# Shorter warm-up products, key weights split by head pair, ScalarE in the centring of Wq, and a later row gather in a gated cross-attention block

## The chip, the cores and the metric

The kernel runs on one core of a Trainium2 chip. The metric is the device time of one execution in microseconds (us); the median of three runs of the kernel before is 1246.3 us (1245.36 to 1249.04). Engines are named as in the profile: PE is TensorE (PEld its weight loads), DVE is VectorE, ACT is ScalarE, POOL is GpSimd, SP issues most of the DMAs.

## The reference

`x` has 4 batches of 2048 tokens of 512 features, all in float32. The context has 77 keys of 384 features for each batch, and there are 16 heads of 64.

```
q = split_heads(layernorm(x) @ Wq);  k, v = split_heads(ctx @ Wk), split_heads(ctx @ Wv)
attn = softmax(q k^T / 8)                      # over 77 keys
x = x + tanh(g_xattn) * ((attn @ v) @ Wo + bo)
idx = argmax(log_softmax(logits) - log(-log(u)))      # one of 8 matrices, chosen from data
x = x + tanh(g_ffn) * (layernorm(x) @ W[idx] + b[idx])
```

## The kernel before

The 8192 tokens are cut into 16 groups of 512. Attention is rearranged so that nothing of width 1024 is made for each token: for each batch a matrix `m` (Wq of a head times the keys of that head) gives the scores straight from the 512 features, and a matrix `vo` (the values of a head times Wo) gives the output straight from the softmax weights. Every large product of a group (`ps_s` scores, `ps_a` attention output, `ps_f` the feed-forward) is done with seven block products in place of eight (class `Seven`, its matmuls are line 466); POOL forms the sums and differences of blocks that this needs (`weight_sum` line 123 for the weights, `Columns.sum` line 437 for the tokens).

Ahead of the 16 groups stands a setup stage, and all of the change lies in it. The order of every engine's queue is written out by hand, in program order; PSUM is a ring of seven banks (`bank`), so that a product can start only when the bank used seven allocations earlier has been copied out. The setup runs on PE in this order:

- three products of a zeroed tile with itself (`ps_w`, line 167), which need no input;
- the keys, `project_k`: for each of 8 head pairs three matmuls over 384 features and 308 columns (4 batches of 77 keys), `ps_kv`, line 270; ACT copies each result out (line 275). Beside it `centre_wq` takes the mean of each row of Wq away: DVE sums a row (line 287), scales the sum (288) and writes half of the centred matrix (295), POOL writes the other half (293). The first half (`wqp[0]`) is used by the next step, the second half 20 us later;
- `build_m(0)`: 32 matmuls (`ps_m`, line 300), each with two copies out (lines 306 and 307), half of the heads by ACT and half by DVE;
- the values, `project_v` (`ps_kv` again): 24 matmuls of 320 columns, because the keys were first copied into a tile `cT` padded with zeros to 80 keys a batch; one copy out each (line 280), by ACT and DVE in turn. Between them stand the small steps that choose the feed-forward matrix: `gates0`, `gates1` and `gates2`, the last of them 12 small DVE instructions (lines 229 to 241) that end in the row numbers `rows_u`;
- `build_m(2)` like the first, then `build_vo` for head pairs 0 to 2 (`ps_vo`, line 336, copied out by ACT and DVE, lines 339 and 341) and the stores of `m` and `vo` to DRAM through SP;
- the score products of group 0. In between stands `mean_wf` (line 659), one product that needs the sum of the four chosen row blocks of W.

These row blocks come by `gather` (lines 246 to 251): five indirect DMAs that POOL issues once `rows_u` is there, behind the three block sums of `m` (line 123). `sum_wf` (lines 623 to 625) adds them up on POOL, behind the scaling of `bf_r` (line 251), which waits for the last of the five.

Weights of keys are loaded in four DMAs of 256 columns each, alternately from ACT's and SP's queue; SP then loads Wq in eight DMAs, Wv in four, and x. There are eight completion semaphores for these DMAs, used in turn, so that the ninth DMA is issued only when the first has landed.

Of the kernel before, what the change touches and what calls it, by code (L numbers as in the profile page):

```python
# [8 lines left out]
F32 = mybir.dt.float32  # L9
U32 = mybir.dt.uint32  # L10
AF = mybir.ActivationFunctionType
ALU = mybir.AluOpType
AX = mybir.AxisListType

P = 128
# [4 lines left out]
def flamingo_block_kernel(  # L20
# [33 lines left out]
    nc = tc.nc  # L54
    NT, D = x.shape
    CD, BJ = ctxT.shape
    ID = WqT.shape[0]
    OPS = b.shape[0]
    B = 4
    J = BJ // B  # L60
    H = 16
    DH = ID // H
    NP = H // 2
    NA = 4
    HA = H // NA
    R = 32 // HA
    NK = 2 * ((J + 2 * R - 1) // (2 * R))
    KH = NK // 2
    JP = NK * R
    BP = B * JP  # L70
    NDC = D // P
    NCC = CD // P
    T = 512
    T2 = T // 2
# [6 lines left out]
    wp = ctx.enter_context(tc.tile_pool(name="work", bufs=1))  # L81
# [6 lines left out]
    def bank(name):  # L88
        return pm.tile([P, 512], F32, tag="mm", name=name)
# [10 lines left out]
    tq = cp.tile([P, 4, NDC // 2, T2], F32, tag="tq")  # L100
# [13 lines left out]
    def flat(t):  # L114
        n = len(t.shape) - 1
        names = " ".join("abcdef"[:n])
        return t.rearrange(f"p {names} -> p ({names})")
# [14 lines left out]
    def row_tile(name):  # L132
        return wp.tile([P, NG, P], F32, tag="row", name=name, bufs=3)
# [1 line left out]
    def column_tile(name):  # L135
        return wp.tile([P, NDC, T], F32, tag="xc", name=name, bufs=3)

    cT = wp.tile([P, NCC, B, JP], F32, tag="row", name="cT", bufs=3)
    s_f = flat(wp.tile([P, HA, NG, JP], F32, tag="s", name="m_st"))
    cR = s_f[:, : NCC * BJ].rearrange("p (c b j) -> p c b j", c=NCC, b=B)  # L140
    wv = snap.rearrange("p (c f) -> p c f", c=NCC)
    wk = m_f[:, 4 * 2 * KH * P :][:, : NCC * ID].rearrange("p (c f) -> p c f", c=NCC)
    t = wp.tile([P, NK * T + KH * T2], F32, tag="pT", name="wq")
# [8 lines left out]
    def load(i):  # L152
        xg[i] = row_tile("xg")
        for a in range(NA):
            nc.sync.dma_start(out=xg[i][ts(a, 32)], in_=rows_of(x, i)[:, :, ts(a, P)])

    def load_ctx(c, queue):
        queue.dma_start(out=cR[:, c].rearrange("p b j -> p (b j)"), in_=ctxT[ts(c, P), :])

    def load_w(t, w, h, queue):  # L160
        queue.dma_start(out=t[:, :, ts(h, ID // 4)], in_=w[:, ts(h, ID // 4)].rearrange("(c p) f -> p c f", p=P))

    nc.vector.memset(tq[:, 0], 0.0)
    idle = tq[:, 0].rearrange("p n t -> p (n t)")
    for _ in range(3):
        ps = bank("ps_w")
        nc.tensor.matmul(ps, idle[:, :P], idle, start=True, stop=True)  # L167
    load_ctx(0, nc.sync)
    load_ctx(2, nc.scalar)
    load_ctx(1, nc.sync)  # L170
    load_w(wk, Wk, 0, nc.scalar)
    load_w(wk, Wk, 1, nc.sync)
    load_w(wk, Wk, 2, nc.scalar)
    load_w(wk, Wk, 3, nc.sync)
    nc.gpsimd.memset(cT[:, :, :, J:], 0.0)
    for c in range(NCC):
        nc.vector.tensor_copy(cT[:, c, :, :J], cR[:, c])
    for p in range(NP):
        nc.sync.dma_start(out=wq[:, p, :], in_=WqT[ts(p, P), :])
    for h in range(4):  # L180
        load_w(wv, Wv, h, nc.sync)
    load(0)
    load(1)

# [43 lines left out]
    def gates2():  # L228
        nc.vector.tensor_scalar(z, z, st[:, 2:3], None, ALU.subtract)
        nc.vector.tensor_tensor(z, z, l2, ALU.subtract)  # L230
        nc.vector.tensor_reduce(st[:, 3:4], z, AX.X, ALU.max)

        nc.vector.tensor_scalar(ez, z, st[:, 3:4], None, ALU.is_equal)
        nc.vector.tensor_tensor(ez, ez, rev, ALU.mult)
        nc.vector.tensor_reduce(st[:, 4:5], ez, AX.X, ALU.max)
        nc.vector.tensor_scalar(st[:, 5:6], st[:, 4:5], -1.0, float(OPS), ALU.mult, ALU.add)
        nc.vector.tensor_scalar(st[:, 6:7], st[:, 5:6], float(D), None, ALU.mult)
        nc.vector.tensor_scalar(st[:, 7:8], st[:, 5:6], float(NA), None, ALU.mult)
        nc.vector.tensor_scalar(rows[:, :NDC], rows[:, :NDC], st[:, 6:7], None, ALU.add)
        nc.vector.tensor_scalar(rows[:, NDC:], rows[:, NDC:], st[:, 7:8], None, ALU.add)  # L240
        nc.vector.tensor_copy(rows_u, rows)
    def gather():
        t = row_tile("wfr").rearrange("p g j -> p (g j)").rearrange("p (c d) -> p c d", c=NDC)
        for c in range(NDC):
            at = bass.IndirectOffsetOnAxis(ap=rows_u[:, c : c + 1], axis=0)
            nc.gpsimd.indirect_dma_start(out=t[:, c, :], out_offset=None, in_=W, in_offset=at)
        at = bass.IndirectOffsetOnAxis(ap=rows_u[:, NDC:], axis=0)
        nc.gpsimd.indirect_dma_start(out=bf_r, out_offset=None,
                                     in_=b.rearrange("o (a j) -> (o a) j", j=P), in_offset=at)
        nc.gpsimd.tensor_scalar(bo_c, bo_c, tgx, None, ALU.mult)  # L250
        nc.gpsimd.tensor_scalar(bf_r, bf_r, tgf, None, ALU.mult)
        return t
# [6 lines left out]
    vT = [v_cols(p, 0, BP).rearrange("p (r b k) -> p r b k", b=B, r=R) for p in range(NP)]  # L259
# [3 lines left out]
    kT_f = kT.rearrange("p n b k r -> p n b (k r)")  # L263
    nc.gpsimd.memset(kT_f[:, :, :, J:], 0.0)

    def project(w, p, keys):
        n = keys.shape[2] * keys.shape[3]
        ps = bank("ps_kv")
        for c in range(NCC):
            nc.tensor.matmul(ps[:, :n], w[:, c, ts(p, P)], keys[:, c].rearrange("p b j -> p (b j)"),  # L270
                             start=(c == 0), stop=(c == NCC - 1))
        return ps[:, :n]

    def project_k(p):
        nc.scalar.copy(kT_f[:, p, :, :J], project(wk, p, cR).rearrange("p (b j) -> p b j", b=B))

    def project_v(p):
        d = vT[p].rearrange("p r b k -> p b k r")
        copy = nc.vector.tensor_copy if p % 2 else nc.scalar.copy
        copy(d, project(wv, p, cT).rearrange("p (b k r) -> p b k r", b=B, r=R))  # L280


    wqp = [wp.tile([P, 2, NP, P], F32, tag="xc", name="wqp", bufs=3) for _ in range(2)]
    wqm = cp.tile([P, NP], F32, tag="wqm")

    def centre_wq(p):
        nc.vector.tensor_reduce(wqm[:, p : p + 1], wq[:, p, :], AX.X, ALU.add)
        nc.vector.tensor_scalar(wqm[:, p : p + 1], wqm[:, p : p + 1], -1.0 / D, None, ALU.mult)
        for h in range(2):
            src = by_chunk(wq[:, p, :])[:, ts(h, 2)]  # L290
            dst = wqp[h][:, :, p, :].rearrange("p q (a e) -> p q a e", a=NA)
            if h:
                nc.gpsimd.tensor_scalar(dst, src, wqm[:, p : p + 1], None, ALU.add)
            else:
                nc.vector.tensor_scalar(dst, src, wqm[:, p : p + 1], None, ALU.add)

    def m_head(q, h, stage):
        p, r = h // 2, ts(h % 2, DH)
# [28 lines left out]
    def build_vo(p, engines):  # L327
        n = 0
        for c in range(3):
            r = min(P, BP - c * P)  # L330
            for hh in range(2):
                stg = stage_of(2 * p + hh)
                hr = ts(hh, DH)
                ps = bank("ps_vo")

                nc.tensor.matmul(ps, v_cols(p, c * P, P)[hr], wo[hr, p, :], start=True, stop=True)  # L336
                src, dst = by_chunk(ps[:r, :]), chunked(stg[:r, c, :])
                if engines[n % len(engines)] == "D":
                    nc.vector.tensor_scalar(dst, src, tgx[:r], None, ALU.mult)
                else:  # L340
                    nc.scalar.activation(dst, src, AF.Copy, scale=tgx[:r])
                n += 1
        for hh in range(2):
            d, stg = vo_d[2 * p + hh], stage_of(2 * p + hh)
            nc.sync.dma_start(out=d[0 : 2 * P].rearrange("(c r) e -> r c e", r=P), in_=stg[:, 0:2])
            nc.sync.dma_start(out=d[2 * P :], in_=stg[: BP - 2 * P, 2])
# [257 lines left out]
              (m_f[:, 4 * 2 * KH * P :], vo_f, vo_f[:, NP * D :], s_f)]  # L604
    wo = wq_f.rearrange("p (n e) -> p n e", n=NP)
    norms[0] = Norms(0)
    for p in range(NP):
        project_k(p)
        centre_wq(p)
    nc.gpsimd.dma_start(out=gg[:, 0:1], in_=g_xattn.partition_broadcast(P))  # L610
    nc.gpsimd.dma_start(out=gg[:, 1:2], in_=g_ffn.partition_broadcast(P))
    nc.gpsimd.dma_start(out=lg, in_=logits.partition_broadcast(P))
# [17 lines left out]
    for p in range(NP):  # L630
        project_v(p)
        if p == 0:
            x_columns(0)
            for t in ("T1", "T2", "T3", "T4"):
                xc[0].sum(t)
            weight_sum(m, 0)
        if p == 2:
            gates0()
        if p == 3:
            gates1()  # L640
        if p == 4:
            norms[0].stats(xg[0], 0, 0, NG)
        if p == 6:
            gates2()
    build_m(2, stages[2:])
    store_m(2, stages[2])
    for n in range(1, 4):
        weight_sum(m, n)
    wfr = gather()
    build_vo(0, "AD")  # L650
    store_m(3, stages[3])
    for p in range(1, 3):
        build_vo(p, "AD")

    wf_mean = wf_f[:, ds(5 * D, D)]

# [30 lines left out]
    n = norms[0]  # L687
# [114 lines left out]
    for i in range(1, NGRP):  # L802
        j, f, nx = i - 1, i - 2, i + 1
        n = norms[i]
# [128 lines left out]
        for s in range(6):  # L933
# [16 lines left out]
            if 2 <= s:  # L950
                k = (0, 2, 3, 5, 6)
# [5 lines left out]
    j, f = NGRP - 1, NGRP - 2  # L957
    n = norms[NGRP] = Norms(NGRP)
# [76 lines left out]
    for s in range(6):  # L1035
# [23 lines left out]
        if s == 5:  # L1059
            f_rows(j, ff, 0, 0)  # L1060
            t = by_feature(ts_[j], 0, 0)
# [50 lines left out]
```

## Time and profile before

| | |
|---|---|
| runs of before | 1245.36, 1246.3, 1249.04 us |
| the profiled execution's own time | 1246.03 us |
| its span, first to last instruction | 1244.2 us |
| PE busy | 1234.0 us, 99% of the span |
| setup up to the first score product | 57.8 us |
| HBM traffic | 64 GB/s over the span; 284 GB/s in the first 36 us |

The profile is that of one execution. In a timeline row the first number is the start in us from the beginning of the span, the second the time that the merged instructions took together; the bracket at the end names the idle time before them and what ended it. In the chain of work the pieces follow one another without a gap: that is the path that sets the end. Each float32 matmul of the program appears as two records on PE.

### The profile page before, as it was taken

The page shows a single profiled execution, that of the slowest core. Times are in us where ns is not written, and L with a number is a line of the kernel's source. Part 1 is how long each engine was busy: PE and PEld are TensorE (multiplying, and loading weights), DVE is VectorE, ACT ScalarE, POOL GpSimd, SP SyncE. Part 2 cuts the span into 40 slices and gives each one's busy share as a digit, 9 for nine tenths or more (in the row PEclk, how much of TensorE's full clock was granted, in tenths as well). Part 3 has the DMA queues.
Part 4 walks back from the last instruction along what each step waited for, and adds up shares of the span by engine and source line. Part 5 has one row for each costly group of instructions (what it writes and reads, how often), then busy time and mean ns, then how long its engine had stood idle before and what let it go on. Part 6 is the DMA issues. An engine that isn't in the chain of part 4 may idle for free.

```text
span 1244.2 us, 16997 instructions
## 1 busy us (share of the span) xinstructions
PE 1234.0 (99%) x5704; PEld 1063.7 (85%) x5704; DVE 907.3 (73%) x1850; ACT 683.4 (55%) x1957; POOL 895.4 (72%) x486
## 2 busy tenths in 40 slices
PE   9999999999999999999999999999999999999997
PEld 6686888888888888888888888888888888888886
DVE  6778976666977766677776767776776877666576
ACT  4639545638274563827356382745638274563824
POOL 5558885857957785685968778575976877585766
PEclk9999999999999999999999999999999999999999
DMA  9868200314024030304106030212304121010102
GB/s 268 300 203 274 57 1 1 68 43 111 1 50 103 1 68 1 68 22 112 20 1 153 1 68 2 47 22 85 68 1 111 43 51 18 1 35 1 35 1 67
DMA packets 95221, 80.27 MB, mean 65 GB/s; under 512 B 3856, under 2 KB 83088, under 8 KB 95136
## 3 DMA queue, kind: packets, MB, share of 16 engines
q1 hardware_dynamic: 92496, 76.61, 24.1%
q10 hardware_dynamic: 2032, 1.47, 0.4%
q8 instruction: 45, 0.74, 0.3%
q0 software_dynamic: 608, 1.13, 0.2%
q14 instruction: 40, 0.33, 0.1%
HBM read 44.07 MB, written 35.13 MB: 64 GB/s over the span
## 4 chain that ended last, share of the span: by engine, by line
PE 96%; DVE 2%; ACT 0%; POOL 0%; issue 0%; DVEq 0%
PE ps_s L466 39%; PE ps_a L466 37%; PE ps_f L466 15%; PE ps_kv L270 2%; PE ps_vo L336 2%; PE ps_m L300 1%; DVE s L370 1%; PE ps_w L167 0%; ACT t L591 0%; POOL r L398 0%; DVE t L417 0%; DVE r L393 0%; DVE y L417 0%; DVE snap L491 0%; DVE y L587 0%
## 5 line engine op out<-in xcount | busy, mean ns | idle before, releaser
L466 PE MATMUL ps_a<-pT,vo 128*128 128x256 f32 x2240 | 486.2, 379 | 0.0
L466 PEld LDWEIGHTS ps_a<-pT,vo 128*128 128x128 f32 x2240 | 425.6, 190 | 57.9
L537 ACT ACTIVATE s<-s,nmx,up 128x77 f32<-128x77 f32 x1024 | 355.6, 445 | 0.8 <-DVE nmx L531 0.8
L437 POOL TENSOR_TENSOR pT<-pT 128x1280 f32<-128x1280 f32 x64 | 186.0, 2907 | 171.4 <-PE ps_a L466 161.9
L466 PE MATMUL ps_s<-tq,m 128*128 128x256 f32 x1280 | 290.6, 380 | 0.0
L466 PEld LDWEIGHTS ps_s<-tq,m 128*128 128x128 f32 x1280 | 242.6, 190 | 36.1 <-issue 2.3
L472 ACT COPY snap<-ps_s 128x512 f32<-128x512 f32 (+1 forms) x188 | 93.6, 515 | 292.7 <-DVE t L417 130.5
L466 PE MATMUL ps_s<-xc,m 128*128 128x256 f32 x960 | 221.1, 379 | 0.0
L466 PEld LDWEIGHTS ps_s<-xc,m 128*128 128x128 f32 x960 | 182.2, 190 | 27.3 <-issue 1.2
L548 POOL TENSOR_TENSOR s<-s,sm 128x1232 f32<-128x1232 f32 x64 | 145.2, 2271 | 46.7 <-DVE sm L545 46.7
L491 DVE TENSOR_TENSOR snap<-snap,ps_s 128x512 f32<-128x512 f32 (+1 forms) x141 | 83.7, 594 | 130.1 <-PE ps_s L466 125.0
L466 PE MATMUL ps_f<-tq,wf 128*128 128x256 f32 x512 | 118.3, 379 | 0.0
L557 DVE STREAM_TRANSPOSE pT<-s 128x512 f32<-128x512 f32 x160 | 101.0, 678 | 15.6 <-POOL s L548 15.6
L437 POOL TENSOR_TENSOR tq<-xc,tq 128x512 f32<-128x512 f32 x64 | 85.4, 1335 | 35.5 <-PE ps_f L466 33.0
L398 POOL TENSOR_TENSOR r<-r,neghalf 32x16 f32<-32x16 f32 (+1 forms) x33 | 93.2, 2833 | 21.9 <-DVE r L393 21.3
L466 PEld LDWEIGHTS ps_f<-tq,wf 128*128 128x128 f32 x512 | 97.3, 190 | 13.2
L544 DVE TENSOR_REDUCE sm<-s 128x16 f32<-128x1232 f32 x64 | 91.5, 1430 | 20.7 <-ACT s L537 20.7
L520 DVE STREAM_TRANSPOSE s<-snap 128x512 f32<-128x512 f32 x156 | 99.9, 685 | 6.1 <-ACT snap L472 3.8
L529 DVE TENSOR_REDUCE ps_st<-s 128x16 f32<-128x1232 f32 x64 | 92.4, 1444 | 2.1
L466 PE MATMUL ps_f<-xc,wf 128*128 128x256 f32 x384 | 90.7, 379 | 0.0
L437 POOL TENSOR_TENSOR tq<-xc 128x512 f32<-128x512 f32 x64 | 81.6, 1275 | 7.1 <-DVE xc L412 5.8
L472 ACT COPY snap<-ps_f 128x512 f32<-128x512 f32 x63 | 36.9, 586 | 87.8 <-PE ps_f L466 85.2
(138 smaller groups left out, 1187.0 us busy)
## 6 DMA issues: line engine op xcount, KB each, us to landing
xg<-in_x_dram SPq DMA_DIRECT2D x64, 256.0 KB, 6.0
out_dram<-y SPq DMA_DIRECT2D x60, 256.0 KB, 4.1
vo<-vo_d SPq DMA_DIRECT2D x16, 640.0 KB, 6.4
m<-m_d SPq DMA_DIRECT2D x12, 640.0 KB, 4.2
vo_d<-vo SPq DMA_DIRECT2D x14, 512.0 KB, 3.3
m_d<-vo SPq DMA_DIRECT2D x4, 960.0 KB, 5.0
wq<-in_WqT_dram SPq DMA_DIRECT2D x8, 256.0 KB, 6.5
wq<-in_Wo_dram SPq DMA_DIRECT2D x1, 2048.0 KB, 13.8
```

The costliest lines, as they stand in the source:

```text
L270: nc.tensor.matmul(ps[:, :n], w[:, c, ts(p, P)], keys[:, c].rearrange("p b j -> p (b j)"), start=(c == 0), stop=(c == NCC - 1))
L398: nc.gpsimd.tensor_tensor(r, r, neghalf[:32, : r.shape[1]], ALU.pow)
L437: (engine or nc.gpsimd).tensor_tensor(self.at[name], self.at[a], self.at[b_], op)
L466: nc.tensor.matmul(self.ps[r][:, n, :], self.w(blk, c, pair), self.cols(cname, c), start=(first and n == 0 and c == 0), stop=(c == h - 1), ...
L472: nc.scalar.copy(dst, self.ps[r])
L491: nc.vector.tensor_tensor(c, c, self.ps[r], ALU.add)
L520: nc.vector.transpose(key_chunk(sc[i], k), cols.rearrange("p (g h r) -> p g h r", h=HA, r=R))
L529: nc.vector.tensor_reduce(mx, head(i, h), AX.X, ALU.max)
L537: nc.scalar.activation(head(i, h)[:, g, :], head(i, h)[:, g, :], AF.Exp, scale=norms[i].up[:, g : g + 1], bias=nmx[h][:, g : g + 1])
L544: nc.vector.tensor_reduce(sm, head(i, h), AX.X, ALU.add)
L548: nc.gpsimd.tensor_tensor(head(i, h), head(i, h), sums[h].unsqueeze(2).to_broadcast([P, NG, J]), ALU.mult)
L557: nc.vector.transpose(pT[i].all[:, k, :].rearrange("p (g h r) -> p g h r", h=HA, r=R), key_chunk(sc[i], k))
```

## The change

Five edits, all in the setup:

1. The zeroed tile has 256 columns in place of 512, and there are four zero products of 256 columns in place of three of 512.
2. The key weights come in five DMAs (pairs 0, 1, 2-3, 4-5 and 6-7) in place of four of two pairs; one more of them is on ACT's queue.
3. The values are projected from the same unpadded keys, 308 columns. `cT`, its memset and its three copies on DVE go. POOL zeroes the three padded keys of each of the 8 value tiles at the start. Each copy out of values becomes two: 9 chunks of 8 keys (by ACT and DVE in turn) and the last 5 keys, always by ACT.
4. The half of the centred Wq that DVE wrote is written by ACT, three pairs behind the keys: behind the copy of the last keys stand four of the eight.
5. `gates2` and `gather` come behind `build_vo` of pair 2. Before, `gates2` stood among the values and `gather` ahead of `build_vo`.

```
-    nc.vector.memset(tq[:, 0], 0.0)
-    idle = tq[:, 0].rearrange("p n t -> p (n t)")
-    for _ in range(3):
+    idle = tq[:, 0, 0, :]
+    nc.vector.memset(idle, 0.0)
+    for _ in range(4):
         ps = bank("ps_w")
-        nc.tensor.matmul(ps, idle[:, :P], idle, start=True, stop=True)
+        nc.tensor.matmul(ps[:, :T2], idle[:, :P], idle, start=True, stop=True)
...
-    load_w(wk, Wk, 0, nc.scalar)
-    load_w(wk, Wk, 1, nc.sync)
-    load_w(wk, Wk, 2, nc.scalar)
-    load_w(wk, Wk, 3, nc.sync)
-    nc.gpsimd.memset(cT[:, :, :, J:], 0.0)
-    for c in range(NCC):
-        nc.vector.tensor_copy(cT[:, c, :, :J], cR[:, c])
+    load_w(wk, Wk, 0, 1, nc.scalar)
+    load_w(wk, Wk, 1, 1, nc.sync)
+    load_w(wk, Wk, 2, 2, nc.scalar)
+    load_w(wk, Wk, 4, 2, nc.sync)
+    load_w(wk, Wk, 6, 2, nc.scalar)
...
+    K1, R1 = divmod(J, R)
+    for p in range(NP):
+        nc.gpsimd.memset(vT[p][:, R1:, :, K1], 0.0)
 
     def project_v(p):
         d = vT[p].rearrange("p r b k -> p b k r")
+        src = project(wv, p)
         copy = nc.vector.tensor_copy if p % 2 else nc.scalar.copy
-        copy(d, project(wv, p, cT).rearrange("p (b k r) -> p b k r", b=B, r=R))
+        copy(d[:, :, :K1], src[:, :, : K1 * R].rearrange("p b (k r) -> p b k r", r=R))
+        nc.scalar.copy(d[:, :, K1, :R1], src[:, :, K1 * R :])
...
-                nc.vector.tensor_scalar(dst, src, wqm[:, p : p + 1], None, ALU.add)
+                nc.scalar.activation(dst, src, AF.Identity, scale=1.0, bias=wqm[:, p : p + 1])
...
-    for p in range(NP):
-        project_k(p)
-        centre_wq(p)
+    LAG = 3
+    for p in range(NP + LAG):
+        if p < NP:
+            project_k(p)
+        if LAG <= p:
+            centre_wq(p - LAG)
...
-        if p == 6:
-            gates2()
...
-    wfr = gather()
     build_vo(0, "AD")
     store_m(3, stages[3])
     for p in range(1, 3):
         build_vo(p, "AD")
+    gates2()
+    wfr = gather()
```

More of the change, by code (lines that the diff above doesn't have):

```diff
@@ L136, in column_tile @@
         return wp.tile([P, NDC, T], F32, tag="xc", name=name, bufs=3)
-    cT = wp.tile([P, NCC, B, JP], F32, tag="row", name="cT", bufs=3)
     s_f = flat(wp.tile([P, HA, NG, JP], F32, tag="s", name="m_st"))
@@ L158, in load_ctx, with load_w @@
         queue.dma_start(out=cR[:, c].rearrange("p b j -> p (b j)"), in_=ctxT[ts(c, P), :])
-    def load_w(t, w, h, queue):
-        queue.dma_start(out=t[:, :, ts(h, ID // 4)], in_=w[:, ts(h, ID // 4)].rearrange("(c p) f -> p c f", p=P))
-    nc.vector.memset(tq[:, 0], 0.0)
-    idle = tq[:, 0].rearrange("p n t -> p (n t)")
-    for _ in range(3):
+    def load_w(t, w, p0, n, queue):
+        queue.dma_start(out=t[:, :, ds(p0 * P, n * P)],
+                        in_=w[:, ds(p0 * P, n * P)].rearrange("(c p) f -> p c f", p=P))
+    idle = tq[:, 0, 0, :]
+    nc.vector.memset(idle, 0.0)
+    for _ in range(4):
         ps = bank("ps_w")
-        nc.tensor.matmul(ps, idle[:, :P], idle, start=True, stop=True)
+        nc.tensor.matmul(ps[:, :T2], idle[:, :P], idle, start=True, stop=True)
     load_ctx(0, nc.sync)
@@ L180, in flamingo_block_kernel @@
     for h in range(4):
-        load_w(wv, Wv, h, nc.sync)
+        load_w(wv, Wv, 2 * h, 2, nc.sync)
     load(0)
@@ L264, in flamingo_block_kernel, with project @@
     nc.gpsimd.memset(kT_f[:, :, :, J:], 0.0)
-    def project(w, p, keys):
-        n = keys.shape[2] * keys.shape[3]
+    def project(w, p):
         ps = bank("ps_kv")
         for c in range(NCC):
-            nc.tensor.matmul(ps[:, :n], w[:, c, ts(p, P)], keys[:, c].rearrange("p b j -> p (b j)"),
+            nc.tensor.matmul(ps[:, :BJ], w[:, c, ts(p, P)], cR[:, c].rearrange("p b j -> p (b j)"),
                              start=(c == 0), stop=(c == NCC - 1))
-        return ps[:, :n]
+        return ps[:, :BJ].rearrange("p (b j) -> p b j", b=B)
     def project_k(p):
-        nc.scalar.copy(kT_f[:, p, :, :J], project(wk, p, cR).rearrange("p (b j) -> p b j", b=B))
+        nc.scalar.copy(kT_f[:, p, :, :J], project(wk, p))
+    K1, R1 = divmod(J, R)
+    for p in range(NP):
+        nc.gpsimd.memset(vT[p][:, R1:, :, K1], 0.0)
     def project_v(p):
         d = vT[p].rearrange("p r b k -> p b k r")
+        src = project(wv, p)
         copy = nc.vector.tensor_copy if p % 2 else nc.scalar.copy
-        copy(d, project(wv, p, cT).rearrange("p (b k r) -> p b k r", b=B, r=R))
+        copy(d[:, :, :K1], src[:, :, : K1 * R].rearrange("p b (k r) -> p b k r", r=R))
+        nc.scalar.copy(d[:, :, K1, :R1], src[:, :, K1 * R :])
     wqp = [wp.tile([P, 2, NP, P], F32, tag="xc", name="wqp", bufs=3) for _ in range(2)]
```

## The prediction

> **What bounds the kernel now.** I read the page's busy times first, then the chain of waits for the setup, then the timeline at the places that the edits touch, and last the DMA view of two stretches.
>
> ```profile
> PE 1234.0 (99%) x5704; PEld 1063.7 (85%) x5704; DVE 907.3 (73%) x1850; ACT 683.4 (55%) x1957; POOL 895.4 (72%) x486
> ```
>
> PE is busy all the time. So no other engine's work shortens anything by itself: an edit counts only if PE does less, does it at a higher clock, or waits where it did not. The chain says where in the setup:
>
> ```profile
> 0.91 0.50 DVE tq L163
> ...
> 1.45 5.49 PE ps_w L167 x6
> 6.94 12.49 PE ps_kv L270 x48
> 19.43 8.81 PE ps_m L300 x64
> 28.25 13.12 PE ps_kv L270 x48
> ...
> 57.91 21.04 PE ps_s L466 x96
> 78.95 0.86 PE ps_w L659 x2
> ```
>
> Each piece begins where the last one ends; PE never stops from 1.45 on. Two readings matter. The zero products take 5.49 for six records, 0.855 of pitch behind a start of some 0.15 us, while the same 512 columns take 0.43 in L659 (0.86 for two): PE starts at half speed and is at full speed when the keys run (6.94). And key records of 308 columns take 12.49/48 = 0.260 each, value records of 320 columns 13.12/48 = 0.273.
>
> **Zero products and key weights.** The memset of 512 columns took 0.48; with 256 it is about half, so the zeros start near 1.2. Eight records of 256 columns at half speed are 8 x 0.4275 = 3.42 in place of 5.13: they end near 4.75, where they ended near 6.75. What PE can do then depends on the first key weights. Their first DMA took 4.2 from issue to landing (issued 1.2, landed 5.4), so today they wait 1.3 us for PE. The new first DMA has half the bytes in pieces of 512 B instead of 1024 B. The rows nearest to that are the two stretches in which only Wq (2 KB pieces) and only x (512 B pieces) are moved:
>
> ```profile
> DMA packets 1077, 1.93 MB, mean 386 GB/s; under 512 B 121, under 2 KB 148, under 8 KB 1077
> DMA packets 1652, 0.82 MB, mean 182 GB/s; under 512 B 53, under 2 KB 1652, under 8 KB 1652
> ```
>
> 512 B pieces go at half the rate, so half the bytes take as long as the whole did. Bounds: landing at 4.9 (same rate) to 5.4 (half rate); I take 5.3, by the row of 512 B. PE then idles about 0.5 us and runs keys at half speed from 5.3 until the clock comes. By elapsed time since the first product that is 1.2 + 5.49 = 6.7, by work done 7.1 (the idle time added); I take 6.9. In 1.6 us it does 0.8 us of full-speed key work, so the keys end at 6.9 + 12.49 - 0.8 = 18.6, 0.8 earlier. Later key weights cover: pair 1 is due near 7.9 and came by 7.1 before; pairs 2-3 are due near 9.4, behind as many pieces as the third load is now (8.6). Wq lands up to 1.1 later (0.39 MB at 182 in place of 386), hidden, as DVE loses 0.35 of its 1.17 us for each pair.
>
> [...]
>
> **Centring on ACT.** ACT's queue behind the last keys now holds four centring instructions ahead of the first copies of `ps_m`.
>
> ```profile
> 19.47 0.42 ACT L275 COPY wf<-ps_kv 128x308 f32<-128x308 f32 x1 [1.14 <-PE ps_kv L270]
> ...
> 20.20 0.23 ACT L306 COPY m<-ps_m 128x80 f32<-128x80 f32 x1 [0.31 <-PE ps_m L300]
> ...
> 20.35 0.36 ACT L307 COPY m<-ps_m 128x240 f32<-128x240 f32 x1
> ```
>
> ACT has 0.31 idle here, then copies without a pause, a head in 0.54, for as long as PE makes `ps_m` (8.81 for 32 heads, two at a time, 0.55 a pair): it has no reserve to catch up. The trace has no such instruction from SBUF with 256 columns. Nearest rows:
>
> ```profile
> L591 ACT ACTIVATE t<-t,rs 128x128 f32<-128x128 f32 x240 | 73.3, 389 | 0.5
> L476 ACT ACTIVATE snap<-ps_a,bo_c 128x256 f32<-128x256 f32 x96 | 40.3, 470 | 46.3 <-PE ps_a L466 44.6
> ```
>
> Back to back these are 73.3/240 = 0.305 (128 columns) and 40.3/96 = 0.42 (256 columns). I take 0.42, the same width: 1.68 for four. The first copy, due 0.8 after the keys end, comes 0.46 + 1.68 after it, 1.3 late. The eighth head needs the bank of the first: free 1.3 after `ps_m` begins today, wanted 1.65 after, so 0.3 is cover. PE waits about 1.0, and ACT's pace returns none of it. Bounds: 0.5 (0.305 each) to 1.4 (0.50 each). Centred columns themselves are in time: the fifth is wanted 4.4 us into `ps_m`. The removed DVE instructions (L177, L295) save nothing on the path; DVE is what comes free.
>
> **Values.** 48 records by 0.273 - 0.260 = 0.63 us less on PE, on the path. The extra ACT copies of 20 columns (about 0.2 each, as the smallest ACT copies of the trace) stand beside 1.6 us of PE for each pair, with ACT at 0.78 per two pairs; memsets on POOL fall into an idle stretch (0.1 each). Cover gone, the last 0.2 would delay a `ps_m` bank, inside its 0.3.
>
> So at the start of the score products PE is ahead by 0.8 - 1.0 + 0.63 = 0.43 us.
>
> **The later gather.** This is the edit that moves a wait onto the path.
>
> ```profile
> 57.41 2.06 DVE L339 TENSOR_SCALAR vo<-ps_vo,tg 128x512 f32<-128x512 f32 x3 [1.27 <-DMA m_d<-vo]
> ...
> 59.62 1.07 POOL L246 DMA_INDIRECT wfr<-in_W_dram,rows_u  x1 [0.15 <-issue]
> ...
> 72.88 0.61 POOL L251 TENSOR_SCALAR bf_r<-bf_r,tg 128x128 f32<-128x128 f32 x1 [6.79 <-DMA bf_r<-in_b_dram,rows_u]
> ...
> 76.15 1.27 POOL L625 TENSOR_TENSOR wf<-wf,wfr 128x512 f32<-128x512 f32 x1
> ...
> 78.78 1.02 PE L659 MATMUL ps_w<-wf,ones 128*128 128x512 f32 x2
> ```
>
> Today the row numbers are ready at 41.7, and POOL starts the gather at 59.62, behind its block sums. The chain from there has no slack: five issues of 1.25, landing 8.0 behind the last, four POOL instructions, end at 77.42; the product that needs the sum starts at 78.78. Cover: 1.36, less some 0.1 for the semaphore, 1.25. Now DVE computes the row numbers behind the copies of `ps_vo`, which end at 59.47, as POOL's block sums do. The 12 instructions took 39.27 to 41.70 = 2.43 in the trace. So the gather starts 2.43 later against PE's work, and so does `sum_wf`: its landing is between the indirect loads' own extremes, 8.0 and 9.0, since SP's stores of `vo` still run then (-0 to +1.0; an emptier queue could take off up to 0.5, by the small POOL loads' 7.5). PE waits 2.43 - 1.25 = 1.2 us at L659. Behind the waiting product stand the score products of the second column pair; DVE, ACT and POOL follow PE. On POOL, `sum_wf` stands ahead of the power for the norms (L398), and ACT waits for that; those 1.2 us run out before the head maxima, where POOL's 5.2 idle (ahead of the second L398) and ACT's 3.1 lie. What it hides today: DVE is idle for 5.6 us behind 59.47, so the 12 instructions delay nothing of their own engine.
>
> **Sum.** -0.43 + 1.2 = +0.8 us on the profiled execution's 1246.03 gives 1246.8. That execution lies 0.3 under the median shown, so as a median it may as well be 1247.1. I give 1246.9. Bounds of the terms: keys 0.5 to 1.1, ACT 0.5 to 1.4, gather 0.7 to 2.2, hence -0.5 to +1.9: 1245.5 to 1248.
>
> **Rivals.** *The clock comes late (slower).* Half speed ended once, after 5.49 us of unbroken products. The change cuts these to 3.4 us and leaves a hole of about 0.5. If the hole makes PE begin anew, the clock comes 5.49 behind 5.3, at 10.8 in place of 6.9: 3.9 more at half speed cost 1.95, together +2.75: 1248.8. It decides if first key weights land behind the zeros' end, 4.75. For it: 512 B pieces. Against: `ps_w` has only this one row, and a hole of a tenth need not count.
>
> [...]
>
> *The gather costs nothing (faster).* If its landing is shorter by 1.2, as the stores of `vo` have then moved further, PE keeps its 0.43, and with ACT's lower bound 0.9: 1245.1 to 1245.6. For it: stores and gather shared the DMA engines from 65 to 72. Against: SP was still storing `vo` until 76.
>
> *It does not do what it says.* Pair 0 lands no sooner and the zeros are only replaced by idle time: the keys gain 0.5 or nothing, 1247.3 to 1247.7; this is inside the forecast.
>
> **How the numbers follow.** Forecast with the last rival 0.50 (1246.0 to 1248.0); late clock 0.20 (to 1250.2 with the upper bounds); gather hidden 0.16 (down to 1244.3 with the other lower bounds); a cause that I don't see, 0.14, more of it slower. The range 1244.3 to 1250.0 leaves out that last and a part of the late clock. 0.3%, about what a measurement of this kernel can tell from no change (its three runs span that), is 3.7 us: 1242.6 and 1250.0. Faster needs an unseen cause (0.07), slower an unseen cause or the late clock at its worst (0.15), the rest is the same (0.78).
>
> **What would show it.** The chain after: zeros of 3.4 to 3.6 us; first key product near 5.3 and idle time ahead of it; keys ending 0.8 earlier; `ps_m` of the first build near 9.8 instead of 8.81, with ACT's first L306-copy 2.1 behind the last keys; values 12.5; the gather's first issue 2.4 behind DVE's last `ps_vo` copy; PE idle 1.2 ahead of the mean product, released by POOL. Wrong if: key records of double pitch run past 8 us, no wait stands at the mean product, or the first build keeps 8.8.

## The result and the profile after

The changed kernel takes 1247.68 us (median of 22 runs, 1247.2 to 1252.09) against 1245.83 us (22 runs, 1244.96 to 1249.48): 1.85 us more, a ratio of 1.0014 with the interval 1.0008 to 1.0021. That is slower by 0.14%, within the 0.3% called the same above; the forecast was +0.8. The profiled execution after took 1248.69 us with a span of 1246.9, so it lies 1.0 above its own median, and 2.7 above the profiled execution of before.

The page's busy times answer first. PE's busy time is as before within 1 us; the span has grown by 2.7, so PE now stands still where it did not.

```profile
PE 1233.1 (99%) x5706; PEld 1065.3 (85%) x5706; DVE 902.9 (72%) x1839; ACT 685.5 (55%) x1973; POOL 893.6 (72%) x493
```

PE's waits of the whole run (line waited for: us in total, times, longest). Before there was only the wait for the memset, now there are five:

```profile
PE ps_w L665 <- POOL wf L632: 2.5, 1, 2.5
PE ps_kv L268 <- DMA m<-in_Wk_dram: 1.4, 2, 1.0
PE ps_w L168 <- DVE tq L165: 1.2, 1, 1.2
PE ps_s L470 <- ACT snap L476: 0.2, 1, 0.2
```

The chain of waits, which before was PE without a break from 1.45 on (start us, us, what):

```profile
1.66 6.13 DMA m<-in_Wk_dram
7.84 11.15 PE ps_kv L268 x42
18.99 9.43 PE ps_m L304 x64
28.42 12.64 PE ps_kv L268 x48
...
62.18 1.07 POOL wfr L245
...
79.81 1.26 POOL wf L632
81.07 2.90 POOL r L402
...
86.88 0.75 ACT snap L476 x2
87.67 4.69 PE ps_s L470 x20
92.36 2.78 PE ps_vo L340 x12
```

The set-up of keys and values ends a little sooner: the score products start at 57.53, where they started at 57.84. What is new lies behind that. The chain leaves PE at the second `build_m` and goes through POOL's block sums, the gather, `sum_wf`, the power for the norms (L402) and ACT, and comes back to PE only at 87.67. The values of pair 3 (`ps_vo`) begin at 92.36, 3.06 later than before. With the 0.31 that PE was ahead, 3.4 us are lost between the two places.

PE's timeline, then POOL's, show both halves of it:

```profile
1.19 3.41 PE L168 MATMUL ps_w<-tq 128*128 128x256 f32 x8 [1.19 <-DVE tq L165]
5.03 1.79 PE L268 MATMUL ps_kv<-m_st,m 128*128 128x308 f32 x6 [0.43 <-DMA m<-in_Wk_dram]
...
81.12 1.12 PE L665 MATMUL ps_w<-wf,ones 128*128 128x512 f32 x2 [2.48 <-POOL wf L632]
...
87.67 1.13 PE L470 MATMUL ps_s<-tq,m 128*128 128x256 f32 x4 [0.24 <-ACT snap L476]
```

```profile
62.18 1.07 POOL L245 DMA_INDIRECT wfr<-in_W_dram,rows_u  x1 [3.03 <-DVE rows_u L240]
...
76.55 0.60 POOL L250 TENSOR_SCALAR bf_r<-bf_r,tg 128x128 f32<-128x128 f32 x1 [7.92 <-DMA bf_r<-in_b_dram,rows_u]
...
79.81 1.26 POOL L632 TENSOR_TENSOR wf<-wf,wfr 128x512 f32<-128x512 f32 x1
81.03 2.94 POOL L402 TENSOR_TENSOR r<-r,neghalf 32x16 f32<-32x16 f32 x1
```

POOL stands idle for 3.03 until the row numbers come, issues the gather 2.56 later than before, waits 9.1 for the last landing where it was 8.0, and so ends the sum at 81.07 instead of 77.42: 3.65 later. (The chain lists POOL's wait as issue; the timeline shows that it ended with DVE's row numbers.) PE waits 2.48 for it at the mean product. Right behind the sum stands the power, whose input DVE had ready at 76.93.

### The profile page after: what moved, and what is told of

Its sections match the earlier page's. It is cut to its first block, busy times and chain, and to the rows that moved or that the text cites. A ratio compares the mean times of both kernels' runs of the same rounds, so it can differ in the third digit from the quotient of the medians.

```text
span 1246.9 us, 17020 instructions
## 1 busy us (share of the span) xinstructions
PE 1233.1 (99%) x5706; PEld 1065.3 (85%) x5706; DVE 902.9 (72%) x1839; ACT 685.5 (55%) x1973; POOL 893.6 (72%) x493
## 4 chain that ended last, share of the span: by engine, by line
PE 93%; DVE 2%; POOL 2%; issue 1%; ACT 1%; DMA 0%; SPq 0%; POOLq 0%; DVEq 0%
PE ps_s L470 37%; PE ps_a L470 37%; PE ps_f L470 15%; PE ps_kv L268 2%; PE ps_m L304 1%; PE ps_vo L340 1%; POOL m L123 1%; DVE s L374 1%; DMA m<-in_Wk_dram 0%; POOL r L402 0%; ACT t L595 0%; POOL wfr L245 0%; DVE t L421 0%; DVE r L397 0%; DVE y L421 0%
## 5 line engine op out<-in xcount | busy, mean ns | idle before, releaser
L402 POOL TENSOR_TENSOR r<-r,neghalf 32x16 f32<-32x16 f32 (+1 forms) x33 | 93.1, 2831 | 21.8 <-DVE r L397 16.1
```

What stands on the lines that cost most here:

```text
L402: nc.gpsimd.tensor_tensor(r, r, neghalf[:32, : r.shape[1]], ALU.pow)
```

## The experiments

All are timed in rounds beside the kernel before. Line numbers differ a little from kernel to kernel; the names say what is meant.

**Edit 5 taken out, and edit 5 alone.** The first is the changed kernel with `gates2` among the values and `gather` ahead of `build_vo`, as before:

```
-    gates2()
-    wfr = gather()        # behind build_vo(2)
+        if p == 6:
+            gates2()      # in the loop over the values
...
+    wfr = gather()        # ahead of build_vo(0)
```

> The changed kernel with its fifth edit undone: the row numbers are computed among the values and the gather is issued before the vo products, as in the kernel before; edits 1 to 4 stay. Theory G (the loss comes from the gather, the rest is a small gain): PE does not wait at the mean product; it starts the score products 0.3 us ahead of before, as the changed kernel did, keeps that lead to the end, and the time is 1245.0 to 1246.0, 0.1 to 0.25% under the changed kernel. Rival S (edits at the start, key loads and ACT's centring, cost the time and the gather's wait is only where it shows): the time stays near the changed kernel's 1247.7.

Measured: 1245.81 us, ratio 1.0001 (0.9992 to 1.0010), inside the expected range, but not by the expected lead: in the profiled execution the score products start 0.33 later than before, because the second key load came at 8.27 and PE waited 0.88 for it. The mean product has no wait; PE runs through:

```profile
58.24 21.04 PE ps_s L470 x96
79.28 0.86 PE ps_w L666 x2
80.14 9.50 PE ps_s L470 x44
```

The second is the kernel before with edit 5 only.

> The kernel before with the fifth edit alone: the row numbers and the gather behind the vo products. Theory G: the gather starts 2.4 to 2.6 us later against PE, its landing takes 8 to 9.2 us, PE waits 1.2 to 2.5 us at the mean product and some 0.7 us more behind it for a copy of ACT; time 1247.5 to 1249.3. Rival S: below 1246.5.

Measured: 1248.26 us, ratio 1.0022 (1.0012 to 1.0032), with a landing of 8.7. Behind the start of the score products its waits of PE are those of the changed kernel:

```profile
PE ps_w L658 <- POOL wf L625: 1.7, 1, 1.7
...
PE ps_s L466 <- ACT snap L472: 0.2, 1, 0.2
```

So edit 5 by itself makes the loss (2.65 us by the medians here; the interval meets that of the changed kernel), and the other four edits together change nothing that can be measured.

**Which of the two paths behind the gather.** The prediction held that only the mean product waits. Here the changed kernel has that product later, in the next column pair's loop, where it cannot be the first to wait:

```
-        if s == 4:
-            mean_wf()
...
             s_rows(0, 4, s2.chunk(0, 0))
             load(2)
+            mean_wf()
```

> The changed kernel with the mean product (and ACT's copy of it) moved behind the sixth of the seven products of the last column group; the rest as changed. If the wait of PE at the mean product is the whole loss, the 2.5 us of idle PE go and the time falls to 1245.0 to 1246. If the second path, from POOL's sum through POOL's power for the norms and ACT's copies to the bank that a score product needs, holds as well, only some 0.5 to 1.5 us come back, PE waits for ACT's snap copy or in the vo products instead, and the time is 1246.3 to 1247.3.

Measured: 1247.85 us, ratio 1.0019 (1.0010 to 1.0028). Nothing is won, less than either expectation. The wait at the mean product is gone, and another one stands four products later:

```profile
85.64 1.13 PE L470 MATMUL ps_s<-tq,m 128*128 128x256 f32 x4 [1.46 <-ACT snap L476]
```

PE has no free bank there, since ACT's copy of the bank stands in its queue behind the `rs` copies, which wait for POOL's power:

```profile
82.50 0.84 ACT L407 COPY rs<-r 32x16 f32<-32x16 f32 x4 [6.46 <-POOL r L402]
```

That ACT waits for the power, and PE for ACT, was then tested by letting the power go first, with the late gather and the late mean product kept:

```
-        nc.gpsimd.tensor_scalar(bo_c, bo_c, tgx, None, ALU.mult)   # in gather
-        nc.gpsimd.tensor_scalar(bf_r, bf_r, tgf, None, ALU.mult)   # now in sum_wf
...
-            sum_wf(wfr)
         elif s == 1:
             norm_step(n, 1)
+            sum_wf(wfr)
```

> The changed kernel, gather as late as there, but on POOL the power for the norms goes ahead of the scaling of bo_c and bf_r and of the sum of the gathered rows, and the mean product stands as late as in e7_mean_late. Theory (the loss goes through POOL's order: the power, and with it ACT's copies and the bank of a score product, stand behind the landing of the gather): no wait of PE is left between 57 and 92 us and the time is that of e1_gather_back, 1245.4 to 1246.2. Rival (the late gather loads the DMA engines or POOL in another way): the time stays at 1247 or above.

Measured: 1245.79 us, ratio 0.9997 (0.9988 to 1.0006): the loss is gone by the medians, though the gather is issued nearly as late as in the changed kernel (4.41 behind the start of the score products; there 4.65, before 1.78). POOL does the power as soon as DVE has its input, and no wait of PE behind the keys is listed:

```profile
77.11 2.94 POOL L400 TENSOR_TENSOR r<-r,neghalf 32x16 f32<-32x16 f32 x1 [8.94 <-DVE r L395]
```

PE's stretch from the first score product to the values of pair 3 is still 0.37 longer than before (31.76 against 31.39; 34.8 in the changed kernel).

**Centring on DVE again.** The kernel without edit 5, its centring as before (edits 1 to 3 remain):

```
-                nc.scalar.activation(dst, src, AF.Identity, scale=1.0, bias=wqm[:, p : p + 1])
+                nc.vector.tensor_scalar(dst, src, wqm[:, p : p + 1], None, ALU.add)
-    LAG = 3
+    LAG = 0
```

> Edits 1, 2 and 3 alone: the changed kernel with the gather as before and the first half of the centred Wq written by DVE with no lag, as before. Theory: ACT's queue holds nothing between the last keys and the first copies of ps_m, the first build takes 8.8 us in place of 9.43, and the kernel is 0.6 us faster than the one with the gather alone put back: 1244.5 to 1245.4. Rival (ACT's four instructions are covered by the banks): the build takes 9.4 either way and the times are the same.

Measured: 1245.53 us, ratio 0.9997 (0.9988 to 1.0006). The first build is 9.22, between the 8.8 of the theory and the 9.4 of the rival: part of ACT's delay is gone, but with the five key loads Wq arrives later, and with it DVE's centring. The changed kernel's trace shows by how much: its first Wq load is the ninth DMA and is issued at 3.59, behind a wait of 1.0 for a context load (before: 2.66, without a wait), and DVE's first sum starts at 10.97 in place of 9.70. DVE's centring, which ended at 19.16 before, would by that end near 20.4 (an estimate: the same 1.27 later).

**The key loads.** The kernel without edit 5, its key weights in four loads of two pairs:

```
-    load_w(wk, Wk, 0, 1, nc.scalar)
-    load_w(wk, Wk, 1, 1, nc.sync)
-    load_w(wk, Wk, 2, 2, nc.scalar)
-    load_w(wk, Wk, 4, 2, nc.sync)
-    load_w(wk, Wk, 6, 2, nc.scalar)
+    load_w(wk, Wk, 0, 2, nc.scalar)
+    load_w(wk, Wk, 2, 2, nc.sync)
+    load_w(wk, Wk, 4, 2, nc.scalar)
+    load_w(wk, Wk, 6, 2, nc.sync)
```

> e1_gather_back with the second edit undone as well (key weights in four loads of two pairs, alternately from ACT and SP). Theory: the first load lands at 5.4 in place of 5.0, but nothing is missing for the second pair, so the keys run without a gap and end at 17.9 to 18.7 in place of 19.0 to 19.5; 0.5 to 1 us faster than e1_gather_back, 1244.8 to 1245.4. Rival (the gap only moves to a later pair): the same time as e1_gather_back.

Measured: 1245.5 us, ratio 1.0009 (0.9996 to 1.0022), with four of twelve runs from 1247.48 to 1251.39. By the medians, each against its own comparison, it is 0.4 faster than the kernel with the gather alone put back; 0.5 to 1 was expected, and the intervals overlap. The chain has one piece for the keys, without a second hole, and they end at 18.24 (19.47 in the execution of the kernel named in the expectation, 18.90 to 19.14 in four other profiled executions with split loads):

```profile
5.56 12.68 PE ps_kv L267 x48
18.24 9.44 PE ps_m L303 x64
```

**Half of the centring on each.** The last kernel, with pairs 0 to 3 centred by ACT and 4 to 7 by DVE, so that nothing stands in ACT's queue ahead of the copies of `ps_m`:

```
+                if p < 4:
                     nc.scalar.activation(dst, src, AF.Identity, scale=1.0, bias=wqm[:, p : p + 1])
+                else:
+                    nc.vector.tensor_scalar(dst, src, wqm[:, p : p + 1], None, ALU.add)
```

> e5_keys_four_loads with the first half of the centring split: ACT writes pairs 0 to 3 between the copies of the keys, DVE pairs 4 to 7 behind its sums. Neither engine then has anything between the last keys and the copies of ps_m. Expected: the first build 8.8 to 8.9 us in place of 9.43, another 0.4 to 0.6 us off, 1244.2 to 1244.9; under the kernel before by 0.06 to 0.12%. Rival (the build is held by something else): 9.2 to 9.4 and no gain.

Measured: 1244.56 us, ratio 0.9993 (0.9985 to 1.0002). The profiled execution is the longest of its twelve runs, 1250.76 us, and shows two mishaps. The first is the late clock:

```profile
5.50 14.82 PE ps_kv L267 x48
20.32 8.81 PE ps_m L306 x64
```

The same keys took 12.68 from 5.56 in the run before this one. In PE's timeline up to 12 us the two start alike and differ in the count of records, 25 there against 17 here:

```profile
5.50 6.79 PE L267 MATMUL ps_kv<-m_st,m 128*128 128x308 f32 x17 [0.54 <-DMA m<-in_Wk_dram]
```

```profile
5.56 6.72 PE L267 MATMUL ps_kv<-m_st,m 128*128 128x308 f32 x25 [0.60 <-DMA m<-in_Wk_dram]
```

The profile's column of the granted clock says 1.00 for all of this time in both; only the pace of the records tells. The first build takes 8.81: its delay is away when ACT centres nothing behind the keys. The second mishap is told with the last experiment.

**Zeros without a hole.** Two ways to keep PE busy until the first keys are there, both built on the last kernel: three products of 512 columns as before, or five of 256 ("the same" in the second expectation is the kernel of the next experiment). The lines of the second:

```
-    for _ in range(4):
+    for _ in range(5):
```

> e9_split_centre with the first edit undone: three zero products of 512 columns. If the short zero products are worth what the chain says, the keys begin up to 1.3 us later when the clock is late and 0.3 us later when it comes early, at a clock that is nearer to full: 0.2 to 0.8 us slower than e9_split_centre. If only the clock's release counts, the same time.

> The same with the row numbers and the gather where the kernel before has them. Expected: the same median within 0.3 us, 1244.1 to 1244.8. If a slow DVE instruction among the row numbers (as in the profile of e9_split_centre) explains the runs 2 to 6 us above the median, this kernel keeps some and the one with the late row numbers has none.

Measured: 1244.91 us, ratio 0.9994 (0.9986 to 1.0003), and 1244.54 us, ratio 0.9988 (0.9979 to 0.9997), in each case eleven runs with none above 1246.1. In both profiles the first key product follows the zeros without a wait. The medians with and without the hole (1244.56) cannot be told apart by these intervals. Neither this kernel with five zeros nor that with the late gather has a run above 1245.1, so the runs don't say whether the slow instruction explains the long ones.

**All of it with the late gather.** The same two sets of zeros, with the late gather, the power first and the mean product late.

> All that the runs so far point to in one kernel: five zero products of 256 columns (no hole ahead of the first key weights, no overrun), four key loads, values of 308 columns, centring split between ACT (pairs 0 to 3) and DVE (4 to 7), gather as late as in the changed kernel but with POOL's power ahead of it and the mean product late. Expected: no wait of PE between 5.6 and 92 us, 1244.1 to 1244.8, and few runs above 1246. If the late gather still costs something it is 1245 or more.

> As e13_five_zeros_late with three zero products of 512 columns. Expected: 0 to 0.4 us slower than it, by the overrun of the zeros; 1244.4 to 1245.0.

Measured: 1244.46 us, ratio 0.9990 (0.9981 to 0.9999) with five zeros, and 1245.29 us, ratio 0.9997 (0.9988 to 1.0006) with three long ones. The first is with its twin that leaves the gather in its old place the best version, 1.6 us under its comparison by the medians. The two builds (8.81 each) and the values (12.64) have the smallest times of all these runs, as they have with three long zeros; ahead of the keys a hole of 0.31 is left in this execution:

```profile
5.78 12.68 PE ps_kv L265 x48
18.45 8.81 PE ps_m L304 x64
27.27 12.64 PE ps_kv L265 x48
```

The second was 0.8 slower than the first, where 0 to 0.4 was expected. In the profiled executions (1245.85 and 1244.65) the difference lies at the zeros: the three long ones ran at half pace to their end (5.49 for their six records, 0.43 for each of the two of the mean product) and the keys started at 6.94, 1.16 later than with the five short ones; the score products start 1.15 later.

**Two engines at one time.** The second mishap of that long run was one small DVE instruction, on 4 elements a partition (0.23 in the changed kernel), beside a POOL block sum (both rows are from that long run):

```profile
41.68 2.94 DVE L237 TENSOR_SCALAR rows<-rows,st 128x4 f32<-128x4 f32 x1
```

```profile
41.71 2.88 POOL L123 TENSOR_TENSOR m<-m 128x1280 f32<-128x1280 f32 x1 [5.54 <-DMA m_d<-m]
```

Both end together. From the start of the values to the end of the second build that execution took 25.75 us (29.14 to 54.89), where the kernel with five zeros, which differs from it in the zeros alone, took 21.63: the meeting cost 4.1. The first mishap may have brought the second: with the keys ending 1.7 later the row numbers came later too, and the sum, which waits for a store of `m`, did not. In the kernel before, `gates2` ends at 41.70 and that block sum begins at 42.00, 0.3 later. To bring them together on purpose, `gates2` was put one pair later in the kernel before:

```
-        if p == 6:
+        if p == 7:
             gates2()
```

> The kernel before with its 12 row-number instructions one pair later, behind the last copy of values, so that they run while POOL makes the first block sum of m (42.0 to 44.9 us). In the profile of e9_split_centre such an instruction took 2.94 us beside that sum in place of 0.23. If DVE is held out for as long as POOL's sum runs, one of the 12 takes 1 to 2.9 us, DVE's first copies of ps_m in the second build come 4 to 5 us late, and the time is 4 to 5 us above before, 1249.5 to 1250.5. If the slow instruction had another cause, the 12 take 2.43 us, PE waits 2.1 us and the time is 1247.5 to 1248.2.

Measured: 1251.8 us, ratio 1.0047 (1.0033 to 1.0060), the largest effect of all these runs, for one step of one call, and 1.3 above the expected range. The instruction that meets the sum takes 2.52 where it took 0.20, the 12 take 4.76 where they took 2.43, and `build_m` waits for DVE's copies. The 5.8 hold the later place of the 12 as well as the meeting; no run separates the two:

```profile
42.19 2.52 DVE L229 TENSOR_SCALAR z<-z,st 128x8 f32<-128x8 f32 x1
```

```profile
41.79 2.90 POOL L123 TENSOR_TENSOR m<-m 128x1280 f32<-128x1280 f32 x1 [6.18 <-DMA m_d<-m]
```

```profile
PE ps_m L300 <- DVE m_st L307: 3.0, 1, 3.0
```

## Why the prediction was right and wrong

The sign was right, and the cause was the one named: the later gather costs more than the other edits bring. The size, +0.8 for a measured +1.85, was off by the following terms. It lies just inside the stated bound of +1.9; the terms as listed add up to +2.5 (-0.5 + 1.4 - 0.63 + 2.2), and the two profiled executions differ by 2.7, outside both. The lower bound with a hidden gather adds up to 1244.8, not 1244.3.

- **The gather, 1.2 forecast.** It measured 3.4 in the profiled execution. By the medians, each against its own comparison, it is 1.65 (the changed kernel against the same without edit 5) to 2.65 (edit 5 alone). The step that failed is the sentence that the waits on the second path, `sum_wf` ahead of the power and ACT behind it, "run out before the head maxima". It was judged by idle times that come too late (POOL's 5.2 from 81.9 on, ACT's 3.1 from 86.3 on), and not by the ring of seven banks: in the kernel before, the score product that needs ACT's copy starts near 84.8. With the mean product out of the way the time stayed (1247.85); with the power ahead of the sum as well the loss was gone (1245.79). Measured against PE's own progress, the sum came 3.96 later in the changed kernel (3.65 + 0.31) and PE lost 3.4; in the kernel with the late mean, by the same rows, it came 2.5 later and PE lost 2.2. So this path has a reserve of 0.3 to 0.6, where the prediction had set 1.25 for the other path and no limit for this one. The 0.1 that the prediction took off for the semaphore is shown by no row; PE's mean product began 0.05 behind the sum's end in the changed kernel (81.12, 81.07).
- **The gather's start, 2.43 later forecast.** Of the 3.96, the later issue makes 2.87 (62.18 against 57.53, before 59.62 against 57.84) and the longer landing 1.1. DVE's last copies of `ps_vo` wait for a store by DMA in both kernels (1.27 before, 1.70 after), so PE's lead of 0.31 did not reach the row numbers behind them.
- **The landing, 8.0 to 9.0 with 8.0 taken.** It was 9.1, 8.7 and 7.9 in the three kernels that lose time, and 8.1 in that with the power first, whose gather is late too; with an early gather it was 8.0 in the kernel before, 8.1 with the gather alone put back and 7.9 with the centring on DVE. So the late gather landed up to 1.1 us later in two of these four kernels, and in the other two not. That the profiled execution of the changed kernel had a long one fits its lying 1.0 above the median; this is argued, since the other runs have no trace.
- **First key load, 5.3 taken of 4.9 to 5.4.** It landed at 4.9, and the hole is 0.43. The rate of 512 B pieces was read from a stretch with x alone (182 GB/s). Here they made 303 GB/s between 3.6 and 4.4 us, against 381 for the 1024 B pieces of the kernel before in the same stretch (the second row; both hold the end of the context loads too). They lost a fifth, not a half:

```profile
DMA packets 467, 0.24 MB, mean 303 GB/s; under 512 B 22, under 2 KB 467, under 8 KB 467
```

```profile
DMA packets 304, 0.30 MB, mean 381 GB/s; under 512 B 16, under 2 KB 304, under 8 KB 304
```

  The landing came at the lower of the prediction's two bounds, 4.9, the one with the same rate for both sizes. That the rate is the same, these two rows do not show.
- **"Later key weights cover" was wrong.** Pair 1 landed at 7.8, and PE waited 1.0 for it. In the kernel before pair 1 was part of the first load, there at 5.4; the prediction's 7.1 belongs to the second load, pairs 2 and 3. The split made pair 1 the second load, and that landed at 7.7 to 8.3 in five kernels; the second load of two pairs, twice the bytes, was there by 7.1 in the kernel before. The keys gained 0.44 instead of 0.8; with loads of two pairs the wait is not there. Why half the bytes come no sooner is open.
- **Centring on ACT, 1.0 forecast.** The four instructions took 1.70 (forecast 1.68) and the first copy came 2.0 behind the start of `ps_m` (forecast 2.1), but the first build took 9.43 instead of 8.81, 0.62 more: a term rightly built, with its cover too small by 0.4. With ACT's part of the centring done ahead of the last keys the build is 8.81.

```profile
19.34 1.70 ACT L299 ACTIVATE wqp<-wq,wqm 128x256 f32<-128x256 f32 x4
20.95 0.21 ACT L310 COPY m<-ps_m 128x80 f32<-128x80 f32 x1
```

- **Values, 0.63 forecast.** They took 12.64, 0.48 less; 48 records in 12.64 are 0.263 each, not the 0.260 of the keys. The ahead-by-0.43 at the score products came out as 0.31 (keys 0.44, build -0.62, values 0.48): the errors cancelled.
- **The late clock** was a true rival. In the changed kernel's profiled execution the keys ran at full pace from the first, but in the long run with the split centring each microsecond from 6 to 10 us touches three key records and the one from 10 to 11 five, and the keys took 2.1 more than in the run before it. The full pace also comes at different times without any hole: the same three zero products, which took 5.49 in the profile before, took 4.38 in the kernel with edit 5 alone and 4.96 in that with long zeros, with the keys right behind them:

```profile
1.45 4.38 PE ps_w L167 x6
5.83 12.44 PE ps_kv L270 x48
```

```profile
1.45 4.96 PE ps_w L168 x6
6.41 12.44 PE ps_kv L267 x48
```

  So the 5.49 from which the rival was priced was one draw of several, and differences of up to 1.1 us (5.49 against 4.38) in the setup of two single executions can be the pace of PE's first records alone. What sets the moment at which the full pace comes, no run shows. Whether the hole makes long runs more frequent is not shown: no run of the 22 with five zeros lay above 1245.1, and several kernels with a hole of about 0.5 had single runs above 1250, but the kernel with edit 5 alone, without a hole, had one of 1251.03, and the kernel before one of 1249.48. Their causes were not seen in a trace.
- **The gather costs nothing** is refuted by the kernel with edit 5 alone, and **it does not do what it says** was right for one part: the earlier keys were given back to the second load.

No run separates the two moved calls, `gates2` and `gather`. By the rows it is `gates2`: POOL has the same order in both kernels, block sums and then the gather, and what it waits for in the changed one is the row numbers (3.03). This is argued, not tested.

## What to carry to other kernels

When a step is moved later, follow every instruction that stands behind it in its engine's queue, and not only the one that uses its result: here a power of 2.94 us for another purpose happened to be queued behind the late sum, and in the kernel with the late product this alone cost PE 2.2. Moving the product alone won nothing; moving it and putting the power first took the loss away. The power first with the product in its old place was not run. Read the reserve of such a path from the buffers that the busy engine needs next, not from the next idle time of the engines in between. And of a load that is cut up, look at each piece's due time: the first came earlier as meant, and the wait for the second gave most of that back.

## What the runs showed of the hardware

In two profiled executions a small DVE `TENSOR_SCALAR` on SBUF that met a POOL sum on SBUF lasted until the sum ended: 2.52 instead of 0.20 where `gates2` stood one pair later, and 2.94 instead of 0.23 in the long run with the split centring, both ending with a sum of 2.9. The kernel before has it already, at an instruction that takes 0.45 in place of 0.20 (the time of the same shape in L229) and ends at 33.00, with a sum that ends at 32.97; in the changed kernel it takes 0.41 and ends at 32.95 (the sum: 32.93), in that long run 0.48 and 33.74 (33.71). The reduction ahead of it, beside the same sum, took 0.17 here as in those two:

```profile
32.32 0.17 DVE L218 TENSOR_REDUCE st<-lg 128x1 f32<-128x8 f32 x1
32.55 0.45 DVE L219 TENSOR_SCALAR z<-lg,st 128x8 f32<-128x8 f32 x1
```

```profile
31.70 1.27 POOL L437 TENSOR_TENSOR tq<-xc,tq 128x512 f32<-128x512 f32 x1
```

By what means the sum holds DVE, no run shows. Not every meeting made the DVE instruction longer: beside POOL's scaling of `bf_r` (76.55 to 77.15 in the changed kernel) a DVE `TENSOR_SCALAR` of 32x16 took 0.18. DVE's copies out of PSUM went on beside such a sum: in the kernel before, those that began between 42.2 and 44.9, beside the sum from 42.00 on, took 0.24 and 0.37 to 0.40, where those of the first build took 0.24 and 0.40. There 0.3 us lie between the row numbers and that sum (41.70 and 42.00). One meeting cost some 4 us (25.75 against 21.63), and nothing but the order of unrelated steps keeps the distance.
